# A fold by row-shifting matmuls replaced by SBUF-to-SBUF transfers and GpSimd adds, with the reads of a patch spread over columns

## The chip, the cores and the metric

The kernel runs on one core of one Trainium2 chip, in fp32. The metric is the device time of one execution in microseconds (us). The engines are called as the profile calls them: PE is TensorE, DVE is VectorE, ACT is ScalarE, POOL is GpSimd, and SP is SyncE, which only issues transfers (DMAs). A transfer is issued from the queue of SP, ACT or POOL.

## The reference, cut to what matters

Two layers of "outlook attention" on a map of 8 images of 56 x 56 pixels with 384 channels; the change concerns layer 0. Each pixel has, for each of 12 heads, a 9 x 9 table of weights (softmax over its last index): it mixes the 3 x 3 neighbours' values into 9 outputs, and each output is added to the pixel that lies at its own place in the 3 x 3 neighbourhood (the fold).

```
v = x @ Wv.T                                   # layer 0, x is group-normalised
v_unf = nine shifted copies of padded v        # b, n, 9 (q), heads, d
a = softmax((x @ Wa.T).reshape(b, n, heads, 9, 9) * d ** -0.5, axis=-1)
out = einsum('bnhpq,bnqhd->bnphd', a, v_unf)   # 9 (p) outputs of each pixel
for i in range(3):
    for j in range(3):
        canvas[:, i:i + h, j:j + w] += out[:, :, :, 3 * i + j]
y = canvas without its border @ Wo.T           # added to x
...                                            # layer 1: the same with one 9-vector a head, and no fold
```

The kernel doesn't build `out`. Since all of it is linear in v, it first adds the weights that join the same pair of pixels: for each output pixel a window of 5 x 5 source pixels. These summed weights are what the fold makes.

## The kernel before

**Tiling.** The 8 images are taken as four pairs, and a pair is a grid of 112 rows (two images of 56, `R`) by 56 columns. Layer 0 goes through it column by column, 224 columns in all. In a column the partitions are the 112 rows. The output side works on patches of 7 columns, 8 in a pair, 32 in all.

**A column.** `attend` makes the logits of one column with three groups of matmuls into three PSUM banks (`bank<-wa_t,xn`). DVE takes the maximum and subtracts it (L550, L551), ACT takes the exponential (L555), DVE sums the denominator, inverts it and zeroes it where a row lies outside the image (L567 to L573), and POOL multiplies the weights `at` by it (L574). Every column but one in eight also projects one tile of values v (`bank<-wv_t,xn`), which ACT copies and writes to the table `vtab` in DRAM (L317).

**The fold.** `presum` adds the weights along the columns (`pre`, on POOL, L593 to L597): weights of column c-1, c and c+1 that reach the same window. `fold` adds them along the rows. A row is a partition, so the shift by one row up and down is a matmul with a shifted identity, `shift`, into the PSUM tile `pw`. ACT copies its two outer entries into `wt`, and DVE adds the three inner ones to the unshifted part:

```
for qi in (0, 2):
    matmul(pw[:, 2 - qi : 2 - qi + K, :], shift[:, qi, :], pre[:, :, qi, :], ...)
nc.scalar.copy(mid[:, 0 : E0 : E0 - 1, :], pw[:, 0 : E0 : E0 - 1, :])
nc.vector.tensor_tensor(mid[:, 1 : 1 + K, :], pw[:, 1 : 1 + K, :], pre[:, :, 1, :], ALU.add)
```

ACT then writes `wt` to the table `ztab` in DRAM, once for each of the one or two patches that the column belongs to (L625).

**A patch.** Once the columns of a patch and its two neighbours on each side are written, SP reads `vp` (values, from `vtab`, `fetch_v`), then `z` (summed weights, from `ztab`), one of each for each of the two images, and `xres` (the residual) in `fetch`. `contract` multiplies `vp` with `z` (`pc`), ACT copies the result to `yT`, `project_out` multiplies by Wo (`po`), DVE adds the residual to `x1t` and takes its statistics, and SP stores it.

**What sets the order.** Matmuls and the instructions of an `InOrder` engine stay in the order in which the program is written; the others are placed by a scheduler. The loop over steps is written out by hand: in step s come `presum` of column s-2, `attend` of column s, and between the three parts of `attend` one job of the list `jobs`, `fold` of column s-3, and another job. The jobs are the contractions (4 for a patch) and projections (6) of patches that have been read; they carry a step from which they are due. A patch's `vp` is read at the end of a step, `z` and `xres` one step later, and its jobs are due four steps after that. `upkeep` brings the statistics of the next pair of images (loads `xr`, transposes, stores `xT`), zero fills of the tables, and loads and normalises the next columns (`xin`, `xn`). Layer 1 (`layer1`) begins with the last patch of layer 0 still to be done (`last_of_layer0`); its own buffers lie where layer 0's were.

DMAs of SP and ACT signal on eight semaphores that are used in turn, and a DMA waits until the one before it on its semaphore has landed.

Of the kernel before, what the change touches and what calls it, by code (L numbers as in the profile page):

```python
# [8 lines left out]
F32 = mybir.dt.float32  # L9
# [6 lines left out]
def two_outlook_layers(  # L16
# [133 lines left out]
    gmat = const.tile([P, NCH, C], F32, name="gmat")  # L150
    with tc.tile_pool(name="ps_setup", bufs=2, space=PS) as ps_setup:
# [10 lines left out]
        for i in range(NCH):  # L162
            pg = ps_setup.tile([P, C], F32, tag="pg", name=f"pg_{i}")
            matmul(pg, gsel[:, i * P : (i + 1) * P], gsel, start=True, stop=True)
            nc.vector.tensor_scalar_mul(gmat[:, i, :], pg, 1.0 / GC)


    shift = const.tile([R, K, R], F32, name="shift")
    gpsimd.memset(shift, 0.0)
    for k in range(-1, 2):  # L170
        s = shift[:, k + 1, :]
        gpsimd.affine_select(
            out=s, in_=s, compare_op=ALU.not_equal, fill=1.0,
            base=k, pattern=[[-1, R]], channel_multiplier=1,
        )
    for b in range(1, IMG):
        gpsimd.memset(shift[:, 2, b * H : b * H + 1], 0.0)
        gpsimd.memset(shift[:, 0, b * H - 1 : b * H], 0.0)


    PH_ALL = K * HEADS0
    inside = const.tile([R, K, PH_ALL], F32, name="inside")
    gpsimd.memset(inside, 1.0)
    for b in range(IMG):
        for pi, row in ((0, b * H), (2, b * H + H - 1)):
            gpsimd.affine_select(
                out=inside[:, pi, :], in_=inside[:, pi, :], compare_op=ALU.not_equal, fill=0.0,
                base=-row, pattern=[[0, PH_ALL]], channel_multiplier=1,
            )

    NZERO = (EP0 - E0) * ROW0
# [23 lines left out]
    def clear_weights(table, line, part, sx, slot, row, first, e, ep):  # L215
# [4 lines left out]
        fill(table, top + (first + e) * row, [[line, R], [slot, sx]], (ep - e) * row)  # L220
# [18 lines left out]
    def row_on_all(src, n, name):  # L239
        t = const.tile([P, n], F32, name=name)  # L240
        nc.scalar.dma_start(t, src.rearrange("(o n) -> o n", o=1).to_broadcast([P, n]))
        return t
# [9 lines left out]
    def norm_params(st, name, params, key):  # L252
# [3 lines left out]
        def over_groups(src, what):  # L256
            pg = ps.tile([P, NCH, IMG], F32, tag="t", name=f"p{what}_{name}")
            for j in range(NCH):

                near = [i for i in range(NCH) if abs(i - j) < 2]  # L260
                for i in near:
                    matmul(
                        pg[:, j, :], gmat[:, i, j * P : (j + 1) * P], src[:, i, :],
                        start=(i == near[0]), stop=(i == near[-1]),
                    )
# [102 lines left out]
    ba_t = row_on_all(ba1, NA1, "ba1_t")  # L368
    bv_t = row_on_all(bv1, C, "bv1_t")
# [27 lines left out]
    def layer0(late, pools):  # L397
# [6 lines left out]
        stats, st1s, params, xins, attns, pres, xrs, xts = {}, {}, {}, {}, {}, {}, {}, {}  # L404
# [11 lines left out]
        def stats_chunk(pair, blk, i):  # L416

            if blk == 0 and i == 0:
                stats[pair] = stat.tile([P, NCH, IMG, NBLK, 6], F32, tag="st0", name=f"st0_{pair}")
# [17 lines left out]
        def keep_block(pair, blk):  # L437

            tc.keep_in_program_order(
                nc.sync.dma_start(  # L440
                    xTs[pair][:, :, blk * XB * R : (blk + 1) * XB * R],
                    xts.pop((pair, blk)).rearrange("p i m r -> p i (m r)"),
                )
# [37 lines left out]
        sync = InOrder(nc.sync)  # L481
# [16 lines left out]
        for wt in wts:  # L498
            nc.vector.memset(wt, 0.0)
# [40 lines left out]
        def attend(pair, c, between):  # L540
# [3 lines left out]
            at = work.tile([R, K, K2, PH], F32, tag="at", name=f"at_{nm}", bufs=4)  # L544
# [28 lines left out]
            nc.vector.tensor_mul(den, den, inside)  # L573
            nc.gpsimd.tensor_tensor(at, at, den.unsqueeze(2).to_broadcast([R, K, K2, PH]), ALU.mult)  # L574
            attns[pair, c] = at

        def presum(pair, c):


            pre = work.tile([R, K2, E0, HEADS0], F32, tag="pre", name=f"pre_{pair}_{c}")  # L580

            def of(t, f, n):
# [4 lines left out]
                a = a.rearrange("r pi (qi qj) (pj h) -> r (pi qi) qj pj h", qj=K, pj=K)  # L587
                return a[:, :, 1 - t, f - 1 - t : f - 1 - t + n, :]

            def put(f, n, *terms):  # L590
                dst, terms = pre[:, :, f : f + n, :], [t for t in terms if t is not None]
                if not terms:
                    nc.gpsimd.memset(dst, 0.0)  # L593
                elif len(terms) == 1:
                    nc.gpsimd.tensor_copy(dst, terms[0])
                else:
                    nc.gpsimd.tensor_tensor(dst, terms[0], terms[1], ALU.add)  # L597
# [3 lines left out]
            put(2, 1, pre[:, :, 2:3, :], of(1, 2, 1)) if c + 1 < W else None  # L601
# [3 lines left out]
            pres[pair, c] = pre  # L605

        def fold(pair, c):


            pre = pres.pop((pair, c)).rearrange("r (pi qi) f h -> r pi qi (f h)", qi=K)  # L610
            pw = ps.tile([R, E0, E0 * HEADS0], F32, tag="f", name=f"pw_{pair}_{c}")
            for qi in (0, 2):
                matmul(
                    pw[:, 2 - qi : 2 - qi + K, :], shift[:, qi, :], pre[:, :, qi, :],
                    start=(qi == 0), stop=(qi == 2), skip_group_check=True,
                )
            wt = wts[c % NWT]
            mid = wt[:, :, SX0 - E0 : SX0, :].rearrange("r e f h -> r e (f h)")
            nc.scalar.copy(mid[:, 0 : E0 : E0 - 1, :], pw[:, 0 : E0 : E0 - 1, :])  # L619
            nc.vector.tensor_tensor(mid[:, 1 : 1 + K, :], pw[:, 1 : 1 + K, :], pre[:, :, 1, :], ALU.add)  # L620

            for px, sx in patches_of(c, 2):
                lo = SX0 - 1 - sx
                at = sx * SLOT0 + FIRST0 * ROW0
                nc.scalar.dma_start(  # L625
# [4 lines left out]
        def fetch_v(pair, px):  # L630

            vps[:] = [patch_tiles(f"0_{pair}_{px}", b) for b in range(IMG)]
# [470 lines left out]
```

## Time and profile before

| what | us |
|---|---|
| three runs | 3528.59, 3530.42 (median), 3541.08 |
| the profiled execution: time, span | 3516.74, 3514.6 |
| layer 0's columns, by the span | about 80 to 2312 |
| layer 1, with its end | about 2312 to 3514.6 |

In the profile, the lines of a group name the source line, the engine, the operation, the tiles as out<-in, and the shapes; then the busy time in us, the mean of one in ns, and the idle time of the engine just before them with what ended it. PE's matmuls overlap, so the time that one takes from PE is read from start to start. A row of a table of stages gives the stretch, then for each engine the busy us and (in brackets) the instructions, the granted PE clock, the busy share of the 16 DMA engines, and the GB/s that they moved. A DMA's time to landing is from its issue to the signal that it is done. "Lnnn" is a line of the kernel before; PE's matmuls all have L119, a helper's line, and are told apart by their tiles.

### The profile page before, as it was taken

The page shows a single profiled execution, that of the slowest core. Times are in us where ns is not written, and L with a number is a line of the kernel's source. Part 1 is how long each engine was busy: PE and PEld are TensorE (multiplying, and loading weights), DVE is VectorE, ACT ScalarE, POOL GpSimd, SP SyncE. Part 2 cuts the span into 40 slices and gives each one's busy share as a digit, 9 for nine tenths or more (in the row PEclk, how much of TensorE's full clock was granted, in tenths as well). Part 3 has the DMA queues.
Part 4 walks back from the last instruction along what each step waited for, and adds up shares of the span by engine and source line. Part 5 has one row for each costly group of instructions (what it writes and reads, how often), then busy time and mean ns, then how long its engine had stood idle before and what let it go on. Part 6 is the DMA issues. An engine that isn't in the chain of part 4 may idle for free. (4 is left out here: it accounts for less than half of the span.)

```text
span 3514.6 us, 72311 instructions
## 1 busy us (share of the span) xinstructions
PE 3427.7 (98%) x29014; PEld 2353.0 (67%) x29014; DVE 1935.8 (55%) x4680; ACT 1173.3 (33%) x2727; POOL 1202.1 (34%) x1833
## 2 busy tenths in 40 slices
PE   7899999999999999999999999988999999999998
PEld 5577777777777777777777777655666666666665
DVE  6666666667666676667766666633333333333331
ACT  4333223333333233333322223223434434343432
POOL 2543434434344344344443444331222222221220
PEclk8999999999999999999999999999999999999998
DMA  8999988688886878887757776676878787878775
GB/s 270 286 288 282 275 275 267 212 256 253 279 263 209 272 221 273 259 252 256 236 181 226 245 225 193 222 271 192 226 221 234 217 229 219 243 205 237 216 219 147
DMA packets 672893, 839.34 MB, mean 239 GB/s; under 512 B 302190, under 2 KB 566574, under 8 KB 668462
## 3 DMA queue, kind: packets, MB, share of 16 engines
q1 hardware_dynamic: 321422, 537.46, 47.9%
q10 hardware_dynamic: 323872, 210.54, 22.7%
q0 software_dynamic: 27264, 86.73, 7.5%
q8 instruction: 228, 3.74, 0.5%
q14 instruction: 107, 0.88, 0.1%
HBM read 512.95 MB, written 321.66 MB: 237 GB/s over the span
## 5 line engine op out<-in xcount | busy, mean ns | idle before, releaser
L119 PE MATMUL bank<-wa_t,xn 128*112 128x288 f32 x4032 | 1086.9, 409 | 11.4 <-ACT v L562 7.8
L574 POOL TENSOR_TENSOR at<-at,den 112x972 f32<-112x972 f32 x224 | 504.6, 2253 | 1193.1 <-DVE den L573 1137.8
L119 PEld LDWEIGHTS bank<-wa_t,xn 128*112 128x112 f32 x4032 | 693.4, 177 | 263.7 <-issue 34.3
L119 PE MATMUL po<-yT,wo_t 128*128 128x448 f32 (+1 forms) x2304 | 817.5, 494 | 5.3 <-DVE x1t L685 4.8
L119 PEld LDWEIGHTS po<-yT,wo_t 128*128 128x128 f32 x2304 | 432.8, 191 | 293.5 <-issue 185.4
L119 PE MATMUL pc<-z,vp 121*32 121x49 f32 (+1 forms) x17664 | 487.9, 254 | 25.3 <-DMA vp<-vtab 10.4
L119 PEld LDWEIGHTS pc<-z,vp 121*32 121x32 f32 (+1 forms) x17664 | 441.3, 131 | 103.3 <-issue 79.5
L550 DVE TENSOR_REDUCE mx<-bank 112x36 f32<-112x324 f32 x672 | 327.6, 487 | 310.6 <-PE bank L119 303.7
L317 POOL DMA_DIRECT2D vtab<-v x392 | 213.1, 547 | 825.3 <-DVE v L132 810.4
L119 PE MATMUL bank<-wc_t,xn 128*128 128x438 f32 x1176 | 478.8, 543 | 5.0 <-DMA wo_t<-in_wo 5.0
L119 PE MATMUL bank<-wv_t,xn 128*128 128x384 f32 x1176 | 417.9, 492 | 0.0
L555 ACT ACTIVATE at<-at 112x972 f32<-112x972 f32 x224 | 227.0, 1014 | 344.9 <-DVE at L551 317.6
L551 DVE TENSOR_TENSOR at<-bank,mx 112x324 f32<-112x324 f32 x672 | 328.8, 489 | 21.1 <-DVE mx L550 0.5
L119 PEld LDWEIGHTS bank<-wc_t,xn 128*128 128x128 f32 x1176 | 214.0, 191 | 174.8 <-issue 162.4
L119 PEld LDWEIGHTS bank<-wv_t,xn 128*128 128x128 f32 x1176 | 219.5, 190 | 139.6 <-issue 18.7
L619 ACT COPY wt<-pw 112x120 f32<-112x120 f32 x224 | 58.0, 259 | 654.0 <-PE pw L119 591.2
L597 POOL TENSOR_TENSOR pre<-at,at 112x108 f32<-112x108 f32 (+1 forms) x440 | 238.0, 541 | 110.4 <-DVE wt L620 96.0
L567 DVE TENSOR_TENSOR d<-at 112x432 f32<-112x432 f32 x224 | 141.7, 632 | 204.7 <-ACT at L555 204.7
L132 DVE TENSOR_TENSOR lgt<-bank,ba_t 128x54 f32<-128x54 f32 x196 | 41.7, 213 | 361.3 <-PE bank L119 361.3
L132 DVE SCALAR_TENSOR_TENSOR x1t<-po,bo_t,x1t 128x448 f32<-128x448 f32 (+1 forms) x156 | 97.7, 626 | 248.9 <-PE po L119 248.9
L664 ACT COPY yT<-pc 128x294 f32<-128x294 f32 x256 | 103.4, 407 | 368.9 <-PE pc L119 325.9
L535 ACT ACTIVATE xn<-xin,bias,scale 128x224 f32<-128x224 f32 x336 | 172.9, 566 | 67.2 <-PE bank L119 36.0
(100 smaller groups left out, 2924.6 us busy)
## 6 DMA issues: line engine op xcount, KB each, us to landing
z<-ztab SPq DMA_DIRECT2D x64, 2352.0 KB, 18.0
vp<-vtab SPq DMA_DIRECT2D x64, 1536.0 KB, 8.3
ztab<-wt ACTq DMA_DIRECT2D x336, 183.8 KB, 6.8
vp<-vtab SPq DMA_DIRECT2D x64, 945.0 KB, 12.0
xres<-xT SPq DMA_DIRECT2D x32, 1176.0 KB, 10.1
xin<-xT ACTq DMA_DIRECT2D x54, 672.0 KB, 7.3
z<-ztab SPq DMA_DIRECT2D x128, 258.4 KB, 4.5
x1t<-x SPq DMA_DIRECT2D x26, 1176.0 KB, 19.0
```

What stands on the lines that cost most here:

```text
L119: tc.keep_in_program_order(nc.tensor.matmul(*args, **kwargs))
L132: return lambda *args, **kwargs: tc.keep_in_program_order(op(*args, **kwargs))
L317: queue.dma_start(bass.AP(table.tensor, table.offset + first, [[line, rows], [(R + GAP) * line - PX * C, n], [1, C]],), v.unsqueeze(1).to_ ...
L535: nc.scalar.activation(to[:, i, :, rows], xin[:, i, :, rows], AF.Identity, bias=bias[:, i, b : b + 1], scale=scale[:, i, b : b + 1],)
L550: nc.vector.tensor_reduce(mx[:, pi, :], pl.rearrange("r q a -> r a q"), AX.X, ALU.max)
L551: nc.vector.tensor_tensor(at[:, pi], pl, mx[:, pi, :].unsqueeze(1).to_broadcast([R, K2, PH]), ALU.subtract)
L555: nc.scalar.activation(at, at, AF.Exp, scale=SCALE0)
L567: nc.vector.tensor_add(d4, at[:, :, 0:4], at[:, :, 4:8])
L574: nc.gpsimd.tensor_tensor(at, at, den.unsqueeze(2).to_broadcast([R, K, K2, PH]), ALU.mult)
L597: nc.gpsimd.tensor_tensor(dst, terms[0], terms[1], ALU.add)
L619: nc.scalar.copy(mid[:, 0 : E0 : E0 - 1, :], pw[:, 0 : E0 : E0 - 1, :])
L664: nc.scalar.copy(yT[:, :, :, b, rows_of], pc.rearrange("p i n y m -> p i m (n y)"))
```

## The change

1. **The fold.** `presum` writes `pre` into one of two fixed tiles, as rows of entries with zeroed gaps (`pre_t`). SP then issues two SBUF-to-SBUF transfers, `moved`: the part that goes one row up and the part that goes one row down, each 112 rows of 180 numbers. `fold` no longer uses PE, ACT or DVE: three adds on POOL put `moved` and the own part together in `wt`. It now stands at the beginning of the step, after the next column's `presum`. SP instead of ACT writes `wt` to `ztab`.
2. **Rows outside the image.** The shift matrix had removed terms that cross from one image to the other; now the weights are multiplied by a product `share` of the inverse denominator and a wider mask `inside` (324 numbers a row, in one buffer).
3. **The reads of a patch.** They are spread over six columns, `vp` and `z` of the first image, `vp` and `z` of the second, and `xres`, all on SP in program order. The jobs are due one step after the last z read is issued, the contractions one in a step.
4. **Around it.** `po` alternates between two PSUM tags, one of them `pw`'s. `at` has five buffers (four before). POOL's instructions of `presum` and `fold` and SP's transfers of layer 0 are kept in program order. To make room, `gmat` keeps only the blocks that are used, zero fills use a shorter source in two parts, two tiles of statistics have one buffer, and `shift` and `bv_t` are made at the start of layer 1. The last patch's reads and jobs are spread over layer 1's first steps.

```diff
-    inside = const.tile([R, K, PH_ALL], F32, name="inside")
+    inside = const.tile([R, K, K, PH], F32, name="inside")
...
+        pre_t = [fixed.tile([P, K * (K + 1) - 1, E0 * HEADS0], F32, name=f"pre_{n}") for n in range(NWT)]
+        moved_t = [fixed.tile([P, 2, K, E0 * HEADS0], F32, name=f"moved_{n}") for n in range(NWT)]
+        for t in wts + pre_t + moved_t:
+            nc.vector.memset(t, 0.0)
...
-            at = work.tile([R, K, K2, PH], F32, tag="at", name=f"at_{nm}", bufs=4)
+            at = work.tile([R, K, K2, PH], F32, tag="at", name=f"at_{nm}", bufs=5)
...
-            nc.vector.tensor_mul(den, den, inside)
-            nc.gpsimd.tensor_tensor(at, at, den.unsqueeze(2).to_broadcast([R, K, K2, PH]), ALU.mult)
+            share = work.tile([R, K, K, PH], F32, tag="share", bufs=1, name=f"share_{nm}")
+            nc.vector.tensor_mul(share, den.unsqueeze(2).to_broadcast([R, K, K, PH]), inside)
+            weights = at.rearrange("r pi (qi qj) a -> r (pi qi) qj a", qj=K)
+            share = share.rearrange("r pi qi a -> r (pi qi) a").unsqueeze(2)
+            gpsimd.tensor_tensor(weights, weights, share.to_broadcast([R, K2, K, PH]), ALU.mult)
...
             attns.pop((pair, c - 1), None)
-            pres[pair, c] = pre
+            sync.dma_start(moved[:R, 0], whole[1 : 1 + R, :K])
+            sync.dma_start(moved[1 : 1 + R, 1], whole[:R, 2 * (K + 1) :])
 
         def fold(pair, c):
 
-            pre = pres.pop((pair, c)).rearrange("r (pi qi) f h -> r pi qi (f h)", qi=K)
-            pw = ps.tile([R, E0, E0 * HEADS0], F32, tag="f", name=f"pw_{pair}_{c}")
-            for qi in (0, 2):
-                matmul(
-                    pw[:, 2 - qi : 2 - qi + K, :], shift[:, qi, :], pre[:, :, qi, :],
-                    start=(qi == 0), stop=(qi == 2), skip_group_check=True,
-                )
+            own = pre_t[c % NWT][:R, K : K + E0]
+            moved = moved_t[c % NWT][:R]
             wt = wts[c % NWT]
             mid = wt[:, :, SX0 - E0 : SX0, :].rearrange("r e f h -> r e (f h)")
-            nc.scalar.copy(mid[:, 0 : E0 : E0 - 1, :], pw[:, 0 : E0 : E0 - 1, :])
-            nc.vector.tensor_tensor(mid[:, 1 : 1 + K, :], pw[:, 1 : 1 + K, :], pre[:, :, 1, :], ALU.add)
+
+            gpsimd.tensor_tensor(mid[:, :K], moved[:, 1], own[:, :K], ALU.add)
+            gpsimd.tensor_tensor(mid[:, K:], moved[:, 0, 1:], own[:, K:], ALU.add)
+            gpsimd.tensor_tensor(mid[:, 2], moved[:, 0, 0], mid[:, 2], ALU.add)
 
             for px, sx in patches_of(c, 2):
...
-                nc.scalar.dma_start(
+                sync.dma_start(
                     ztab0[(pair * NPX + px) % NTAB][...],
...
                 for t in range(0, NPY0 // n_tile, NC):
                     jobs.add(due, lambda t=t, f=contract: [f(t + n) for n in range(NC)])
+                    due += 1
+            due -= 1
...
-                po = ps.tile([P, 4 * R], F32, tag="o", name=f"po_{nm}_{half}_{j}")
+                po = ps.tile([P, 4 * R], F32, tag="of"[(half * NCH + j) % 2], name=f"po_{nm}_{half}_{j}")
...
+        def reads(step):
+
+            for after, read in (
+                (-1, lambda *a: fetch_v(*a, 0)), (0, lambda *a: fetch_z(*a, 0)),
+                (1, lambda *a: fetch_v(*a, 1)), (2, lambda *a: fetch_z(*a, 1)),
+                (2, lambda *a: line_up(*a, step + 1)), (4, fetch_x),
+            ):
+                pair, c = divmod(step - LAG - PX - 1 - after, W)
+                if 0 <= pair < NPAIR and c % PX == 0:
+                    read(pair, c // PX)
+
         for step in range(NPAIR * W + LAG):
             if 2 <= step < NPAIR * W + 2:
                 presum(*divmod(step - 2, W))
+            if step >= LAG:
+                fold(*divmod(step - LAG, W))
             todo = [lambda: jobs.run(step, 1)] * 2
-            if step >= LAG:
-                todo.insert(1, lambda: fold(*divmod(step - LAG, W)))
...
-            pair, c = divmod(step - LAG - PX, W)
-            if pair >= 0 and c % PX == 0:
-                fetch_v(pair, c // PX)
-            pair, c = divmod(step - LAG - PX - 1, W)
-            if pair >= 0 and c % PX == 0:
-                fetch(pair, c // PX, step + 4)
+            reads(step)
...
             jobs.run(base + step, 1)
-            if step == 0:
-                last_of_layer0(base + step + 5)
+            reads_of_layer0(base + step)
```

## Prediction

> **What bounds the kernel now.** I read the busy table first, then a table of stages (busy time of each engine, granted clock, DMA share), then the tensor engine's order of time, and last the groups and waits of the parts that the diff touches.
>
> ```profile
> PE 3427.7 (98%) x29014; PEld 2353.0 (67%) x29014; DVE 1935.8 (55%) x4680; ACT 1173.3 (33%) x2727; POOL 1202.1 (34%) x1833
> ```
>
> ```profile
> core 0: us, PE busy (x) PEld busy (x) DVE busy (x) ACT busy (x) POOL busy (x), PEclk, DMA share, GB/s
> 80.00:640.00 560.00, 542.58 (x4638) 387.63 (x4637) 379.85 (x942) 174.85 (x348) 247.40 (x344) 0.99 0.88 273
> 640.00:1200.00 560.00, 559.91 (x4991) 402.27 (x4990) 388.06 (x972) 179.32 (x353) 227.31 (x332) 1.00 0.80 252
> 1200.00:1750.00 550.00, 549.23 (x4769) 393.05 (x4768) 380.11 (x953) 175.49 (x345) 219.95 (x320) 1.00 0.79 251
> 1750.00:2312.00 562.00, 556.35 (x5217) 396.83 (x5219) 369.74 (x887) 158.22 (x311) 234.54 (x343) 1.00 0.69 218
> ```
>
> The four rows are layer 0, one for each image pair: 224 columns in 2232 us, 9.96 us each. PE is idle for 24 us of them, most of it in the first. DVE has 32% free, ACT and POOL over half. DMA is the only other full resource, at 0.88 in the first pair. A busy PE proves little by itself, so I looked at starts in the order of time:
>
> ```profile
> 1510.00 1.62 PE L119 MATMUL bank<-wa_t,xn 128*112 128x288 f32 x6
> 1511.46 0.78 PE L119 MATMUL pw<-pre,shift 112*112 112x180 f32 x4
> 1512.07 1.62 PE L119 MATMUL bank<-wa_t,xn 128*112 128x288 f32 x6
> 1513.53 1.86 PE L119 MATMUL po<-yT,wo_t 128*128 128x336 f32 x6
> ```
>
> Each group starts before the one ahead of it has ended, with no releaser in brackets: PE works in a row and nothing paces it from outside. The fold's four pw instructions take 1512.07 - 1511.46 = 0.61 us of its time.
>
> **What the Trainium skill says.** "Perfetto Trace Analysis", Identifying the Most-Contended Engine: matmul busy share doesn't tell the distance to the roofline, since matmuls are pipelined. The trace agrees: four durations of 0.316 us would make 1.26, the starts give 0.61, so I price pw by starts. "DMA: Bandwidth & Descriptors", Issuing engines are not separate DMA queues: transfers from any engine share the same 16 DMA engines; another issuer saves only the issue time. So moving ztab's writes from ACT to SP moves no load. The same page, Queues, rings and completion order: SP and ACT each own a ring on those engines, consumed in order. A small transfer of SP behind a large one of SP must therefore wait. The trace of before has no such small transfer, but the large ones:
>
> ```profile
> z<-ztab SPq DMA_DIRECT2D x64, 2352.0 KB, 18.0
> ```
>
> ```profile
> DMA to landing us min/median/max: 8.8/18.0/23.0
> ```
>
> "GPSIMD Engine Reference", Elementwise: about 2.6 cycles an element for a two-input add. The groups agree: (2253 - 663) / (972 - 216) = 2.1 ns an element, above about 0.2 us fixed.
>
> **The change, part by part.** (1) *Shift matmuls removed.* 224 x 0.61 = 136.6 us off PE, all on the path. The group's waits go with it:
>
> ```profile
> L119 PE MATMUL pw<-pre,shift 112*112 112x180 f32 x896 | 174.5, 316 | 10.2 <-POOL pre L595 10.2
> L619 ACT COPY wt<-pw 112x120 f32<-112x120 f32 x224 | 58.0, 259 | 654.0 <-PE pw L119 591.2 <-DMA vtab<-v 36.2 <-DMA xin<-xT 10.5
> L620 DVE TENSOR_TENSOR wt<-pw,pre 112x180 f32<-112x180 f32 x224 | 76.5, 342 | 24.1 <-ACT wt L619 16.5 <-issue 3.2 <-POOL pre L597 2.4
> ```
>
> Of the 10.2 us, 3.9 are one wait at the end of layer 0, where the last fold is still awaited; I count 6.3 as gained. ACT's 58 us and DVE's 76.5 us lie beside PE: nothing.
>
> (2) *Three POOL adds a column.* 180, 120 and 60 elements at 0.2 us + 2.1 ns: 0.58 + 0.45 + 0.33 = 1.36 us.
>
> ```profile
> L574 POOL TENSOR_TENSOR at<-at,den 112x972 f32<-112x972 f32 x224 | 504.6, 2253 | 1193.1 <-DVE den L573 1137.8 <-DVE gvar L267 11.5 <-ACT yT L664 10.5
> L597 POOL TENSOR_TENSOR pre<-at,at 112x216 f32<-112x216 f32 x220 | 145.9, 663 | 96.5 <-DVE wt L620 96.0
> ```
>
> POOL has now 2.25 for the weights and about 2.1 for presum, so 5.7 us of a column that shrinks to 9.96 - 0.61 = 9.35: hidden, cost nothing, 3.6 us spare. The weights' wider share product (324 elements for 108) costs DVE 489 - 257 = 0.23 us, less than the 0.34 of the add it loses.
>
> (3) *Two moved transfers a column on SP*, 112 rows of 720 bytes each. Queue 10's row in the page (323872 packets, 210.54 MB, 22.7% of 16 engines' 3514.6 us) gives 39 ns for packets of 650 bytes on average; 224 x 39 / 16 = 0.55 us of all 16 engines a column. First pair: 0.88 x 560 = 493, plus 56 x 0.55 = 31, is 524 us of transfers in the 526 us that PE then wants: full. The fullest 70 us stretch in layer 0 had 0.95. At 1.0 nothing is lost, at 0.95 the pair lasts 552, 26 lost; I take 18. The second and third pair: 0.795 x 1110 + 62 = 944 in 1041, 0.91; they fit. The fourth: 0.79.
>
> (4) *POOL's new wait, for moved.* Behind it on POOL stand the weights' product and the next presum; for the product waits DVE, since share has one buffer. moved(c) is issued after presum(c) and read after presum(c+1): 9.35 us later. If it lands later, POOL can slip its 3.6 us, then 9.35 - 2.25 = 7.1 more before DVE must wait to write share: 20 us from issue. The skill's fit on the DMA page (Anatomy of one DMA, 2 us plus size) gives an estimate of 2.2 us for 80 KB alone. Behind a z read: half of the pair's 18, say 9 to 12, plus that. Under 20: nothing, and a gain isn't possible.
>
> (5) *SP as one ordered queue.* It gains 2 moved and 1.5 ztab issues a column at 0.32 us, about 1.1 us; harmless. But z's read waits on SP for the last ztab write to land (median 6.8 us), with the next moved behind it; those 7 us fit in the 9.35. The instruction order shows SP and ACT sharing eight DMA semaphores in turn, so each DMA waits for the eighth before it. With 7 a column instead of 5, ACT's vtab writes wait for DMAs about one column old instead of 1.3 to 1.6. A z read that lands within a column frees it in time.
>
> (6) *Reads spread.* Before, both z reads go at once, three to four columns ahead of their contraction; now each stands about 2 columns ahead of its own, 18.7 us, alone on the queue. Zero to 64 x 1 us lost; I take 64 x 0.15 = 10. Contractions and projections are due one or two in a column, not always two, and po alternates two PSUM tiles: the 4.8 us that PE waited for x1t may go; not counted.
>
> (7) *Ends.* The last fold pays a moved round trip and the adds before layer 1's buffers come free: 3 to 8 us, I take 5. Four more tiles are zeroed on DVE at the start, 2 us. Shift and bv load in layer 1: beside other work.
>
> Sum, against the profiled execution of 3516.7 us: - 136.6 - 6.3 + 18 + 10 + 5 + 2 = 3409. The median of the runs shown is 13.7 above that execution, so I predict 3422.
>
> **The rivals.** *A: slower, by a blocked fold.* moved lies behind z on SP's ring; past 20 us POOL stops, DVE stops at share, PE has no free bank. Price: 64 reads x (landing - 20). The 108 us gained are gone at 20 + 108 / 64 = 21.7 us. At 23, the longest z landing of before: 3422 + 192 = 3614. For it: DMA at 0.91 and above, and SP's waits for ztab. Against: the 18 us belong to two z reads and xres together; one alone took 8.8. Chance 0.12.
>
> *B: DMA becomes the bound beyond the first pair.* If 0.88 were the most that the mix sustains, the first pair takes 524 / 0.88 = 595, 69 lost, and the next two 944 / 0.88 = 1073, 32 lost: 3422 + 51 + 32 = 3505. For it: the reads come as bursts on that mean. Against: a share of 0.92 stood from 220 to 430 us, with PE busy for 209.7 of the 210. Chance 0.12, time about 3480.
>
> *C: no change.* If a column were paced by its chain of DVE, ACT and POOL, PE would only idle where pw was: 3530. The back-to-back starts and POOL's 1193 us idle before the product speak against it. Chance 0.04.
>
> **How the numbers follow.** My forecast has 0.72, with its own range of 3385 (everything hidden: 3393) to 3450. A 0.12, B 0.12, C 0.04. The range of 3385 to 3500 takes in B's middle and leaves A. About 0.5% is what a measurement of this kernel can tell: faster by more 0.84, same 0.04, slower 0.12.
>
> **What would show it.** Right: no pw in layer 0, columns of about 9.35 us, PE idle under 50 us in layer 0, POOL waiting for moved briefly and DVE not for POOL, DMA share about 0.9 after the first pair. Step 3 is wrong if the first pair isn't the weakest; step 4 if DVE waits for the product; step 6 if PE shows waits for z at pc. The prediction is wrong if layer 0's columns exceed 9.7 us.

## The result, and the profile after

The kernel after takes 3569.35 us (median of 4 runs, 3564.01 to 3588.01), the kernel before 3532.11 (median with one more run than above): a ratio of 1.0111, 95% interval 1.0069 to 1.0153. It is **slower by 1.1%** where 3422 us was predicted. The profiled execution has a span of 3562.3 us (before 3514.6) and a mean granted PE clock of 0.965 (before 0.987).

From the busy table of the kernel after:

```profile
PE 3327.1 (93%) x28118; PEld 2238.1 (63%) x28118; DVE 1924.2 (54%) x4464; ACT 1105.4 (31%) x2503; POOL 1486.5 (42%) x2509
```

The 896 shift matmuls are gone (29014 before). PE's busy time fell by 100.6 us, not by 136.6, so by the price of step 1 the other matmuls took 36 us longer. And PE's idle time, span less busy, rose from 86.9 to 235.2 us. Together, 148.3 us more idle time less 100.6 us of work is the 47.7 us that the span grew.

The table of stages of the kernel after, with the stretches and columns of the one shown for before:

```profile
core 0: us, PE busy (x) PEld busy (x) DVE busy (x) ACT busy (x) POOL busy (x), PEclk, DMA share, GB/s
80.00:640.00 560.00, 468.57 (x3861) 321.85 (x3860) 341.13 (x796) 146.02 (x264) 284.69 (x458) 0.91 0.95 264
640.00:1200.00 560.00, 530.79 (x4751) 370.33 (x4750) 378.50 (x909) 158.39 (x293) 293.43 (x488) 0.97 0.95 267
1200.00:1750.00 550.00, 525.07 (x4648) 365.55 (x4647) 371.51 (x901) 159.56 (x294) 286.41 (x483) 0.98 0.94 266
1750.00:2312.00 562.00, 551.87 (x5071) 381.63 (x5070) 391.96 (x877) 150.80 (x270) 324.67 (x539) 0.99 0.88 246
```

PE is idle for 91 us of the first row (17 before), and the first pair has both the lowest clock and, although more bytes have to move, a lower rate than before (264 for 273 GB/s). By the starts of the first maximum of each column, the four pairs last 604, 574, 568 and 522 us; before 546, 570, 570 and 545. So the loss lies in the first pair (58 us), the next two gain nothing (4 us lost, 2 gained), and only the last one gains (24 of the 34 us that its shift matmuls took). Layer 1 with its end takes 10 us more.

What PE waits for, from the waits (us in total, times, longest):

```profile
PE pc L119 <- DMA z<-ztab: 65.0, 13, 10.7
PE pc L119 <- issue: 37.7, 15, 6.4
PE bank L119 <- DVE at L546: 32.0, 8, 11.1
```

Contractions come before their z has landed. Before, in layer 0 (80 to 2312 us), PE's waits in front of pc were these two alone, and none of them was for z:

```profile
PE pc L119 <- issue: 3.8, 5, 1.8
PE pc L119 <- ACT yT L664: 2.0, 2, 1.5
```

POOL's, ACT's and SP's waits of the kernel after:

```profile
POOL wt L132 <- DMA moved<-pre: 325.4, 78, 14.8
ACT at L550 <- POOL wt L132: 96.0, 16, 8.7
SPq L132 <- POOL wt L132: 759.8, 212, 15.0
```

POOL waits for `moved` in 78 of 224 columns, never longer than 14.8 us; SP waits for POOL's fold in nearly every column; and ACT's exponential sometimes stands behind the fold too. The fold is also finished later: counted from the first maximum of its own column, it ends after 39.5 us (median of the 224 columns; 47.5 in the first pair); in the kernel before it ended after 34.9 (33.9).

### The profile page after: what moved, and what is told of

The parts are those of the page before. It is cut to its first block, busy times and chain, and to the rows that moved or that the text cites. A ratio compares the mean times of both kernels' runs of the same rounds, so it can differ in the third digit from the quotient of the medians.

```text
span 3562.3 us, 71372 instructions
## 1 busy us (share of the span) xinstructions
PE 3327.1 (93%) x28118; PEld 2238.1 (63%) x28118; DVE 1924.2 (54%) x4464; ACT 1105.4 (31%) x2503; POOL 1486.5 (42%) x2509
## 4 chain that ended last, share of the span: by engine, by line
PE 64%; DMA 22%; DVE 4%; issue 4%; POOL 3%; ACT 2%; SPq 1%; ACTq 0%; POOLq 0%; DVEq 0%
PE bank L119 34%; PE po L119 17%; PE pc L119 9%; DMA moved<-pre 5%; DMA z<-ztab 4%; DMA ztab<-wt 4%; DMA xres<-xT 2%; PE pt L122 1%; DMA lgtab<-lgt 1%; POOL at L132 1%; DMA vp<-vtab 1%; DMA xT<-xt 1%; PE bank L122 1%; DMA xr<-in_x 1%; DMA at<-lgtab 1%
## 5 line engine op out<-in xcount | busy, mean ns | idle before, releaser
L119 PEld LDWEIGHTS bank<-wa_t,xn 128*112 128x112 f32 x4032 | 702.1, 179 | 303.2 <-issue 53.5
L132 POOL TENSOR_TENSOR at<-at,share 112x972 f32<-112x972 f32 x224 | 504.1, 2250 | 770.1 <-DVE share L569 711.0
L132 POOL TENSOR_TENSOR wt<-moved,pre 112x180 f32<-112x180 f32 x448 | 230.3, 536 | 340.2 <-DMA moved<-pre 325.4
L546 DVE TENSOR_TENSOR at<-bank,mx 112x324 f32<-112x324 f32 x672 | 321.1, 479 | 20.1 <-POOL pre L132 4.5
L119 PEld LDWEIGHTS bank<-wv_t,xn 128*128 128x128 f32 x1176 | 227.0, 194 | 165.0 <-DVE at L546 35.2
L132 POOL TENSOR_TENSOR pre<-at,at 112x108 f32<-112x108 f32 (+1 forms) x440 | 230.6, 545 | 0.0
```

The source lines that it names most:

```text
L119: tc.keep_in_program_order(nc.tensor.matmul(*args, **kwargs))
L132: return lambda *args, **kwargs: tc.keep_in_program_order(op(*args, **kwargs))
L546: nc.vector.tensor_tensor(at[:, pi], pl, mx[:, pi, :].unsqueeze(1).to_broadcast([R, K2, PH]), ALU.subtract)
```

## The experiments

Two theories at first. **Order**: the new wait and the new places in the queues (moved behind z, ztab behind the fold) cost the time. **Load**: the bytes of moved do, wherever they are issued. A third came up on the way: **lateness**, the fold ends later in the column, so ztab's writes, and z, come later than the jobs allow. Where the text says how late a fold ends, it is counted as above. Differences between runs on different chips are taken from the ratios to the kernel before on the same chip.

### What moved costs

**e1_no_moved.**

```diff
-            sync.dma_start(moved[:R, 0], whole[1 : 1 + R, :K])
-            sync.dma_start(moved[1 : 1 + R, 1], whole[:R, 2 * (K + 1) :])
```

> The changed kernel without its two moved transfers a column; the adds of the fold stay and read a zeroed tile, so the terms of the rows above and below are left out of the result. Three theories of where the gain went. Ring: moved stands behind z, vp and xres on SP's ring, POOL waits 325 us for it in all, and everything behind it is late. Load: the 16 DMA engines are full, share 1.0 in the first pair, and 0.55 us more a column lengthens all transfers. Reads: a z read only two columns ahead of its contraction is too late by itself. Ring and Load both expect most of the forecast gain here, 3400 to 3440 us. Reads expects PE to go on waiting for z, 3480 us or more.

3471.68 us, 0.9844 of before (0.9816 to 0.9873). The two transfers cost 0.027, some 94 us: the pairs are 41, 25, 18 and 5 us shorter than in the kernel after. But even without them only 54 of 137 us are gained. The time lies between what Ring and Load expected and what Reads did; the folds still end late, after 37.1 us.

**e2_moved_unread**: moved is sent, but the fold reads another tile.

```diff
-            whole, moved = pre_t[c % NWT], moved_t[c % NWT]
+            whole, moved = pre_t[c % NWT], moved_t[0]
...
-            moved = moved_t[c % NWT][:R]
+            moved = moved_t[1][:R]
```

> The changed kernel with both moved transfers issued as before, but landing in a tile that no fold reads; the fold adds a zeroed tile, so the terms of the rows above and below are left out of the result. The load is kept, POOL's wait is taken away. Ring (POOL's wait is the cost) expects nearly the time of the kernel without moved, 3400 to 3440 us. Load expects no more than a part of it, 3530 us or above. Reads expects 3480 or more with PE waiting for z.

3542.62, 1.0061 (1.003 to 1.0091): 71 us above e1 on the same chip, with no fold that reads what landed. POOL still waits for moved before it writes `pre` again (53 us) and elsewhere, so it isn't free of order. But its folds end after 37.8 us, 0.7 later than e1's (2.8 in the first pair): with little lateness added, about 71 of the 94 us stay. This is what Load expected.

**e9_moved_pool**: both transfers issued by POOL, off SP's queue.

```diff
-            sync.dma_start(moved[:R, 0], whole[1 : 1 + R, :K])
+            gpsimd.dma_start(moved[:R, 0], whole[1 : 1 + R, :K])
...
```

> The changed kernel with one edit: the two moved transfers are issued from POOL's own queue instead of SP's; ztab stays on SP, so ACT waits for nothing new. All the load stays. Wait: moved's place behind z, vp and xres on SP's ring is what costs the 98 us between the changed kernel and the one without moved; it expects POOL's wait for moved to go and 3480 to 3500 us. Load: the added packets cost it on full engines; it expects 3540 us or more.

3572.24, 1.0109 (1.0075 to 1.0143): the time hasn't changed, as Load expected. Yet POOL's wait is gone, as the view of the tile `moved` of e9 shows (who waited for it, and its landing):

```profile
  POOL wt L132: 11.9, 8
...
DMA to landing us min/median/max: 1.9/5.5/11.5
```

12 us of waiting for 325, and the same time: **with POOL's wait for moved gone, nothing is gained.** It doesn't show that the wait was free, because POOL now issues the transfers itself (0.54 us each), and the folds end no earlier than in the kernel after (40.0 us for 39.5).

### The reads and ztab's queue without the new fold

**e3_old_fold** keeps the spread reads, with the old fold by matmuls and ztab written by ACT; **e13_old_fold_ztab_sp** is e3 with ztab's writes from SP, so without the last edit of the diff; shift matmuls, ACT's copy and DVE's add are those of before.

```diff
+            pw = ps.tile([R, E0, E0 * HEADS0], F32, tag="f", name=f"pw_{pair}_{c}")
...
-            gpsimd.tensor_tensor(mid[:, :K], moved[:, 1], own[:, :K], ALU.add)
...
-                sync.dma_start(
+                nc.scalar.dma_start(
```

> Only the second half of the change: the reads spread over six columns and the jobs' new due steps, with the old fold by shift matmuls (copy on ACT, add on DVE, ztab writes from ACT, one PSUM tile for po). Reads expects it slower than before by what PE waits for z, 60 us or more, 3590 us and above. Ring and Load expect no loss: 3515 to 3540 us.

> The old fold by shift matmuls with the spread reads (3526 us by itself), and now the ztab writes issued by SP instead of ACT. Nothing else of the new fold. SP's ring (writes of 336-byte packets in one ring and one ordered queue with the large reads) expects the loss here, 3560 us or more, with longer packets of xres on SP. New fold (POOL's adds come late and hold up what follows) expects 3520 to 3535 us.

e3: 3526.12, 1.0003 (0.9985 to 1.0021); e13: 3537.9, 1.0037 (1.0022 to 1.0051). Spreading the reads by itself costs and brings nothing (in the columns of layer 0 PE never stood idle before pc). Moving ztab to SP costs 12 us by the ratios, between the two forecasts; it is a small difference between two chips, whose intervals only just part. Their queues (packets, MB, share of 16 engines), e3:

```profile
q1 hardware_dynamic: 328238, 537.46, 48.6%
q10 hardware_dynamic: 323872, 210.54, 23.2%
```

and e13:

```profile
q1 hardware_dynamic: 521774, 600.70, 61.4%
q10 hardware_dynamic: 130336, 147.29, 14.6%
```

The same bytes, but the packets of the two queues last 4.2% more of the span together, some 150 us of 16 engines: in the trace the packets of `xres` (3136 bytes, SP) go from 137 to 192 ns once ztab's 336-byte packets share their queue. That raised the DMA share while the same bytes moved in nearly the same time. The likely reading is that **a longer packet is partly a waiting one, and the share counts it as busy**; the traces don't show what a packet waits for.

**e4_old_reads**: the new fold, with the reads of a patch together as before.

```diff
-                (-1, lambda *a: fetch_v(*a, 0)), (0, lambda *a: fetch_z(*a, 0)),
-                (1, lambda *a: fetch_v(*a, 1)), (2, lambda *a: fetch_z(*a, 1)),
-                (2, lambda *a: line_up(*a, step + 1)), (4, fetch_x),
+                (-1, lambda *a: fetch_v(*a, 0)), (-1, lambda *a: fetch_v(*a, 1)),
+                (0, lambda *a: fetch_z(*a, 0)), (0, lambda *a: fetch_z(*a, 1)),
+                (0, fetch_x), (0, lambda *a: line_up(*a, step + 4)),
```

> Only the first half of the change: the new fold with moved, with vp of both images read together at the end of one step and z of both and xres one step later, jobs due four steps after, as before the change. Reads expects the forecast gain, 3420 to 3450 us. Ring expects it worse than the changed kernel, since moved now stands behind two z reads and xres, 18 us: 3600 us or more. Load expects about the changed kernel's 3569 us.

3609.28, 1.0234 (1.0205 to 1.0264), as Ring expected. POOL's, DVE's and PE's waits of e4:

```profile
POOL wt L132 <- DMA moved<-pre: 439.6, 56, 21.5
...
DVE share L569 <- POOL at L132: 253.5, 42, 12.5
...
PE bank L119 <- DVE at L546: 107.1, 45, 10.3
```

Here POOL waits up to 21.5 us at a time for moved, DVE 254 us for POOL at `share` (15 in the kernel after), and PE 107 us for DVE. This is the chain of rival A, which the spread reads with their due times keep away: they are worth about 40 us to the new fold and nothing to the old.

### Four issuers that made a loop (e5 to e8)

These put ztab's writes or moved on ACT's queue: `nc.scalar.dma_start` for ztab in e5, e6 (without moved) and e7 (moved from POOL); for moved in e8.

> The changed kernel with the ztab writes issued by ACT again, as before the change; moved stays on SP. Two theories of the part that isn't POOL's wait. One ring: the load is the same as before the change but for moved, and it is slower because 336 ztab writes of 336-byte packets now share SP's ring with the large reads (packets of xres 187 ns where they took 134). It expects most of the 98 us between the changed kernel and the one without moved plus some of the rest, 3440 to 3480 us. Full engines: what counts is the sum of transfers, the ring doesn't matter. It expects about 3569 us.

> Without the moved transfers (the terms of the rows above and below are left out of the result) and with the ztab writes issued by ACT again: the same transfers on the same rings as before the change, no shift matmuls. One ring expects the whole forecast gain, 3390 to 3410 us. Full engines expects no more than without moved alone, 3472 us.

> moved issued from POOL's own queue, which carries nothing else in layer 0, and the ztab writes from ACT: moved no longer stands behind z. POOL pays about 1.1 us a column for the issues. One ring expects the best time of all whole kernels, 3400 to 3440 us. Full engines expects 3540 us and above, since all the load is still there.

> The changed kernel with moved issued by ACT, ztab writes left on SP. If moved's place behind z is what makes POOL wait, that wait (325 us) nearly goes and 27 us or more of time with it, 3500 to 3545 us. If ACT in its turn stops at moved's semaphores, its instructions come late and PE waits for ACT: 3570 us or more.

The times, in this order: 3759.82 (1.0626, 1.0577 to 1.0675), 3696.93 (1.0448, 1.0409 to 1.0488), 3857.3 (1.0902, 1.0868 to 1.0936), 3724.74 (1.0527, 1.0485 to 1.0569). Neither theory foresaw e5 and e6; e7 lies in the open range of Full engines, but for another reason. For e8 the time of the second branch came true, and ACT does come late: in front of its exponentials it waits 695 us for POOL's fold. The timeline of e6 shows what happens (start, duration, instruction, idle time before):

```profile
1313.03 2.25 POOL L132 TENSOR_TENSOR at<-at,share 112x972 f32<-112x972 f32 x1 [6.38 <-DVE share L569]
...
1317.92 0.33 POOL L132 TENSOR_TENSOR wt<-moved,wt 112x60 f32<-112x60 f32 x1
...
1318.28 0.33 ACTq L625 DMA_DIRECT2D ztab<-wt  x1
1318.66 1.01 ACT L550 ACTIVATE at<-at 112x972 f32<-112x972 f32 x1 [6.11 <-POOL wt L132]
...
1323.71 2.25 POOL L132 TENSOR_TENSOR at<-at,share 112x972 f32<-112x972 f32 x1 [5.46 <-DVE share L569]
```

ACT reaches the write, waits for the fold, and only then takes the exponential of a later column, on which DVE's sums, POOL's product, presum and the next fold depend: one loop through three engines, 10.7 us for this column. So the times of these runs don't tell load from order by themselves; they tell that **ztab could not stay on ACT with this fold**. e5 less e6, with and without moved in this loop, is 63 us, 48 of them in the first pair and 7 in each of the next two, where e6 moves only 230 to 234 GB/s.

### Later jobs

**e10_later_jobs** gives contractions and projections one step more; **e11_no_moved_later_jobs** is that without moved, **e12_moved_pool_later_jobs** with moved from POOL.

```diff
-                (2, lambda *a: line_up(*a, step + 1)), (4, fetch_x),
+                (2, lambda *a: line_up(*a, step + 2)), (4, fetch_x),
```

> The changed kernel with the jobs of a patch due one step later, so that z has one column more to land. Late z: PE's waits at pc (94 us of idle time in layer 0) are a matter of two columns being too few, and go: 3490 to 3520 us. Wait and Load: POOL is behind anyway and delays whatever comes later: 3555 us or more.

> Without the moved transfers (the terms of the rows above and below are left out of the result), and the jobs of a patch due one step later. Late z: of the 83 us by which the kernel without moved missed the forecast, the 51 us of PE's idle time at pc go: 3405 to 3430 us. If z's lateness only moves on with the jobs: 3465 us or more.

> Both: moved from POOL's queue, and the jobs one step later. If Wait and Late z are both right and add up, this is the whole change with its gain, 3420 to 3450 us, faster than the kernel before. If Load is right, 3520 us or more.

e10: 3588.3, 1.0154 (1.0111 to 1.0198). e11: 3494.54, 0.9889 (0.9858 to 0.992). e12: 3546.56, 1.0046 (1.0036 to 1.0057). e10 less e11 is 94 us: moved costs what it cost before, so one step doesn't hide it; two steps weren't tried. Late z missed in e10 and e11, and e12 came out as Load expected. Against e9, e12 ends layer 0 60 us earlier and then loses 28 in layer 1, whose first steps the last patch's jobs now delay. With moved on SP, layer 0 ends only 4 us earlier in e10 than in the kernel after, and no earlier in e11 than in e1.

**e14_no_moved_ztab_pool** (no moved, ztab from POOL), **e15_all_pool** (moved and ztab from POOL, jobs later except the last patch's) and **e16_moved_pool_later_but_last** (the same with ztab on SP). The first edit is ztab's write in e14 and e15, the second stands in `line_up` in e15 and e16:

```diff
-                sync.dma_start(
+                gpsimd.dma_start(
...
+            due -= is_last
```

> No moved transfers (the terms of the rows above and below are left out of the result), and the ztab writes issued by POOL right behind its adds; SP has only the large transfers. SP's ring expects most of the 83 us that were missing without moved: 3395 to 3425 us. New fold expects 3465 us or more. POOL's issues of 560 packets each may cost it more than moved's 0.55 us; if they cost over 2 us, POOL itself gets late and PE waits for z again.

> A whole kernel: moved and ztab both from POOL's queue, jobs one step later in all patches but the last. If SP's ring and queue were the cost, 3420 to 3450 us, faster than before. If the added load on the engines is the cost, 3500 us or more, with the first pair no shorter than in the changed kernel (604 us).

> moved from POOL's queue, ztab on SP, jobs one step later in all patches but the last. The same with the last patch late too had 3547 us and lost 46 us in layer 1, where its jobs held up the others; without that about 3505 us, faster than before by 0.7%, if the last patch's jobs are the cause; 3540 us if not.

e14: 3482.46, 0.9881 (0.9839 to 0.9924). e15: 3492.49, 0.9907 (0.988 to 0.9935). e16: 3498.13, 0.9928 (0.9894 to 0.9961). e14 came out as New fold expected, so freeing SP's queue alone didn't bring what was missing in e1. e15 lies between its two forecasts, with a first pair of 560 us. e16 is near its 3505, and its layer 1 is 29 us shorter than e12's (the forecast counted 46): the last patch's jobs were the cause. Both e15 and e16 are faster than the kernel before on that chip.

### Load alone, and lateness alone

**e17_no_moved_all_pool** is e15 without its moved transfers; **e18_all_pool_again** is e15 itself, both on one chip.

> The best version so far (ztab's writes from POOL's own queue, jobs one step later except the last patch's: 3492.5, where its moved transfers go out too) without the moved transfers, so the fold adds what lies in moved_t (zeroes): its result lacks the terms of the rows above and below. It asks what moved still costs once order and lateness are mended. Theory load (0.55 us of all 16 engines a column still lengthens the first pair and slows every packet): about 3450 to 3465, nearly all of the gain in the first pair, whose DMA share falls to about 0.90. Theory lateness (moved cost only by what stood behind it; that is mended): 3485 to 3495, the same as with moved. And against the version without moved whose jobs are not later (3482.5): if that one still lost to late z, this one is about 25 us shorter and PE's waits for z at pc fall from 90 us to under 40; if not, it is the same.

> The whole kernel with moved and ztab's writes from POOL's queue and the jobs one step later except the last patch's, again, beside the version without its moved transfers on the same chip, so that the two are compared there. Both theories: about 3492, 0.99 of before. If it isn't under 0.995, the gain of the version is not shown.

e17: 3444.86, 0.9729 (0.9699 to 0.976). e18: 3536.51, 0.9983 (0.9968 to 0.9998). Their stages, e17 first:

```profile
80.00:640.00 560.00, 523.43 (x4452) 361.00 (x4451) 392.88 (x909) 160.94 (x295) 397.83 (x607) 0.98 0.97 274
640.00:1200.00 560.00, 555.69 (x4943) 387.02 (x4942) 401.79 (x953) 169.18 (x311) 382.81 (x607) 0.99 0.88 259
```

```profile
80.00:640.00 560.00, 491.28 (x3960) 336.21 (x3959) 385.97 (x846) 151.11 (x276) 438.02 (x666) 0.95 0.94 267
640.00:1200.00 560.00, 540.23 (x4873) 376.78 (x4872) 410.73 (x920) 161.11 (x296) 446.65 (x697) 0.97 0.91 269
```

*Load.* e18 less e17 is 92 us. So moved costs 94, 94 and 92 us (after and e1, e10 and e11, e18 and e17) in three arrangements of queues and jobs, whether POOL waits 325 us for it or 7. In each of them the fold also ends 2.4 to 3.3 us later with moved than without, so by themselves these differences hold some lateness; e2, with 71 us and a fold little later, tells that **most of the price is the load**. What counts is its bytes, or the time that they take, and not the number of its packets, as the pages of e17 and e18 show:

```profile
DMA packets 507672, 839.24 MB, mean 244 GB/s; under 512 B 114127, under 2 KB 385231, under 8 KB 503247
```

```profile
DMA packets 529181, 875.43 MB, mean 248 GB/s; under 512 B 121295, under 2 KB 399567, under 8 KB 524751
```

Issued by POOL, moved adds 21509 packets and 36.2 MB; issued by SP (kernel after and e1) it adds 57350 packets and the same 36.2 MB, at the same price. By pairs the price is 37, 20, 18 and 14 us from e17 to e18. For the first pair the rate fits: 36.2 MB are 9 MB a pair, and 9 MB at e17's 274 GB/s is 33 us. In the second and third pair PE's added idle time (15 and 16 us) stands nearly all in front of pc: there moved costs time through a z that comes late. How far slower transfers and how far the later fold make it late, these two runs don't part. Note that in the first pair e17 has the higher DMA share, 0.97, and is faster: the share doesn't measure room. This last, and the even spread over the pairs, the Load forecast of e17 had wrong (nearly all in the first pair, a share of 0.90); its time was 5 us under the forecast.

*Lateness.* PE's waits for z in e14:

```profile
PE pc L119 <- DMA z<-ztab: 54.3, 14, 10.7
```

and in e17, where the jobs are one step later:

```profile
PE pc L119 <- DMA z<-ztab: 4.8, 1, 4.8
```

From e14 to e17 the ratio falls by 0.015, 53 us, with no moved in either, and PE's idle time in front of pc in the columns of layer 0 falls from 76 to 14 us. The two ran on two chips, so the 53 may be off by half (see the next paragraph). With e9 to e12 on one chip (60 us in layer 0) that is about the price of late z, where it can be bought back. e10 and e11 say that with ztab and everything else on SP it can't; why not is open.

*The chip.* e15 and e18 are one program on two chips: 3492.49 and 3536.51 us, 1.3% apart, where the kernel before differs by 0.5% (3524.19 and 3541.71). In the first pair e15 moved 277 GB/s, e18 267. So the gain of e15 over before was 0.9% on one chip and 0.2% on the other; by the mark that e18's forecast set (a ratio under 0.995) it is not shown; e16 ran only beside e15, and its 0.7% stands under the same doubt. Between chips the text compares ratios, and of kernels with different DMA load a difference under 1% is then not safe. The differences of e1 and e2, of e9 to e12, of e14 to e16, and of e17 and e18 are each from one chip.

## Why the prediction was wrong, step by step

- **Step 1** (- 136.6 us off PE) held as far as PE's work goes, but not all of it was on the path: e17, without moved and with later jobs, is only 87 us shorter than the kernel before in layer 0's columns. What it left out too: a PE that idles is granted less afterwards. The Trainium skill, "TensorE: Matmul & The Clock Gate", Part 1: The HAM clock gate, says that a window of about 3.4 us without work halves PE's clock, until it has been busy for about as long. The trace agrees. A table in steps of 10 us of the kernel after has a gap of 10.7 us (from 198.3) in its first row, and in its second the full clock again, 11 us after the gap's end:

```profile
200.00:210.00 10.00, 0.92 (x42) 0.95 (x46) 1.75 (x4) 0.00 (x0) 0.31 (x1) 0.54 1.06 355
...
220.00:230.00 10.00, 10.00 (x154) 7.35 (x144) 6.22 (x15) 3.73 (x8) 5.48 (x9) 1.00 0.93 290
```

  In the trace PE has 28 gaps of over 3.4 us, before it had 7. An estimate by that page, 21 more gaps of 3.4 us at half speed each, is 21 x 1.7 = 36 us, as much as PE's other work grew. The trace's own record of the clock has it at half for 251 us (94 before), with PE busy in 166 of them (63 before); the 103 us more could cost up to 51. So a gap cost here its own length and, by the estimate, some 1.7 us more on average.
- **Step 2** was right. The three adds, by form:

```profile
L132 POOL TENSOR_TENSOR wt<-moved,pre 112x180 f32<-112x180 f32 x224 | 131.7, 588 | 340.2 <-DMA moved<-pre 325.4 <-issue 12.0 <-DMA ztab<-zeros 2.8
...
L132 POOL TENSOR_TENSOR wt<-moved,pre 112x120 f32<-112x120 f32 x224 | 108.4, 484 | 0.0
...
L132 POOL TENSOR_TENSOR wt<-moved,wt 112x60 f32<-112x60 f32 x224 | 78.8, 352 | 0.0
```

  1.42 us a column for an estimated 1.36. What was left out is *when*: they now stand after the next presum, at the end of a serial chain, and that is the lateness of step 6 (a fold ends after 39.5 us for 34.9).
- **Step 3 is the step that failed.** It priced moved at 18 us, and it costs 92 to 94, some 71 of them with little lateness (e2). Its load was sized well (720-byte packets lasted 40 ns, 39 were taken). The room was not: it was read from the share, 0.88, as if 0.12 were free, while the GB/s of the same row, 273, was already about the most that any kernel here moved in this stretch (277 in e15; shorter stretches reach more, 294 over 70 us in the kernel before). So the first pair is best read as full before the change. And "the second and third pair fit" had no price for a load that fits: 20 and 18 us a pair in e18 against e17, whose PE is busy for 556 of 560 us in the second and so has little idle time to take it up; in e5 against e6, where PE waits for the loop anyway, it is 7. Why a load of 0.9 costs PE time is shown only in part: from e17 to e18 PE's idle time grows by 84 us, 74 of them in the columns of layer 0, of which 37 in front of pc.
- **Step 4** missed in size (325 us, not "briefly"). Its tolerance of 20 us from issue leaves 10.7 us of waiting, and 4 waits are longer, the longest 14.8 us. Its conclusion survives in the main: DVE waits for POOL only 15 us at `share`, and taking POOL's wait away (e9) brings nothing. The fit that it took for 80 KB alone (the Trainium skill, "DMA: Bandwidth & Descriptors", Anatomy of one DMA) is given there for transfers that POOL issues, where moved went out from SP; from POOL (e9) moved took 1.9 us at the least, near the estimate of 2.2, and 5.5 in the median. Rival A is what e4 does, not what the change did.
- **Step 5** called ztab on SP harmless: some 12 us (e13 against e3, on two chips). The coupling of ACT to POOL by shared semaphores, which it also called harmless, may be behind the 96 us that ACT waited for the fold; no run isolates it.
- **Step 6** took 10 us of at most 64 for late z. PE idles 94 us in front of pc in the columns of layer 0, and 50 to 60 us were bought back by later jobs once transfers went out from POOL. The bound was drawn from the distance between reads and jobs alone; the fold's own delay stood in front of it, and so did step 3's load: without moved (e1) the 94 are 31.
- **Step 7**: layer 1 and the end cost 10 us for 5, the start 2 for 2.

Of the rivals, **B** was right that DMA binds the first pair: it said 595 us, and 604 were measured. That the number is so near is luck, for its reason was that the mix sustains no share over 0.88, and shares of 0.94 to 0.97 are held here; the pair is long because packets last longer and PE idles. B had the next two pairs too short, 1073 us for 1142. (Its own sum, 3505, lay outside the stated range; the 3480 beside it has no working.) "Columns over 9.7 us" was given as what would make the prediction wrong; they are 10.2. Where the 137 us went: e17, which has no moved and gives z more time, still gains only 8, 26, 22 and 32 us in the four pairs of about 34 that each could give; the first runs at 274 GB/s against 273 before, about the most seen. So about 49 us of the gain are out of reach for DMA rate and small idle times, moved takes some 92, and late z and the queues the rest, about 30 us: layer 0's columns take 36 us longer than before, not 137 less. This account takes each part from another pair of runs, so only its size is to be trusted.

## What to carry to other kernels

Read the room of the DMA engines from GB/s against the best rate that a long stretch of the same kernel has held, not from one minus the busy share: here a run with a share of 0.97 was faster than one with 0.94. Price every added byte at that rate in a stretch that is full, and give it a price (here over half of that) even where the share says that it fits and PE has no idle time to take it up. When work moves from PE to a slower chain of engines, count how much later its result is, and move the due times of its readers with it, before judging the exchange.

## What was not expected of the hardware

- Small writes on a queue lengthen the packets of the large reads beside them (`xres` 137 to 192 ns) with little lost (some 12 us of 3526).
- POOL as an issuer: moved took 0.56 us to issue, a ztab write 0.83 us, as the trace of e18 has it; POOL had room for both (2082.9 us busy of 3536).
- One program with moved (e15 and e18) differed more between two chips (1.3%) than the kernel before (0.5%); two chips are too few to say why.
- The same moved transfers go in fewer and larger packets from POOL's queue than from SP's (21509 for 57350), at the same price.
- Another issuer moves no load. The Trainium skill, "DMA: Bandwidth & Descriptors", Issuing engines are not separate DMA queues, says that another issuer saves only issue time; e9 and the kernel after agree, at 1.0109 and 1.0111.
